# Splitting the next heads' weights at the ends of steps instead of in the middle of one

## The chip, the core and the metric

The kernel runs on one core of a Trainium2 chip. Its engines work side by side, each from a queue of its own in the order in which the instructions were written: PE (TensorE) multiplies matrices; its weight loads are listed as PEld. DVE (VectorE) and ACT (ScalarE) work element by element and are the ones that read PE's results out of PSUM. POOL (GpSimd) works element by element on SBUF. SP (SyncE) only issues transfers (DMAs) here; ACT and POOL issue some as well. An instruction that waits holds everything behind it in its own queue.

The metric is the device time of one execution in microseconds (us). A profiled execution is measured too, and its trace is where durations come from.

## The reference: what is computed

The input `x` has 4 batches of 512 rows with 512 values. It is normalized row by row (layer norm); attention with 16 heads of size 128 and a feed-forward network with 1408 hidden units both read the normalized rows; the output is the input plus their product:

```python
xn = _layernorm(x, axis=-1)
s = _L0_attn_ref(xn, ...)          # q, k, v per head, causal softmax, z, sum over heads by W_O
g = _silu(_L0_ffn_ref(xn, ...))    # silu(gate) * up, then down
x = x + s * g
```

Only the attention half is touched by the change. Everything is float32.

## The kernel before, in words

**Split operands.** PE is fed in a rounded type (fp32r), which keeps fewer bits than float32. So each operand is held as a pair, a high part and a low part, and a product is made of three matmuls: high x high, low x high, high x low. To *split* a weight tile of 128 x 512 means: ACT copies it into the rounded type (the cast, line 154), and POOL subtracts that from the raw tile to get the low part (line 155). The raw tile comes from HBM into one of four buffers (pool `rawp`, function `stage`, line 150), issued from ACT's queue during the head steps.

**Steps.** The heads are taken in groups of two (`HG = 2`), eight groups. The main loop of line 681 has 64 steps: for each group g, for each batch b (4), for each head i of the group (2). Step n is 8g + 2b + i. In step n, in the order of PE's queue:

- the scores of this head, `sc` (lines 362 to 368), 128 rows at a time. DVE adds the mask and takes the row maxima (line 376), ACT takes the exponentials (line 390), DVE the reciprocals of the row sums (line 393), POOL normalizes (line 396). That is function `softmax`.
- half of the "filling" work: in steps with i = 0 two row blocks of the values `v` (`project_v`, lines 308 and 312, read out by ACT at line 318 and DVE at 319 and 320), in steps with i = 1 two row blocks of the output projection of the previous batch (`project_out`, lines 93 to 95, read out by DVE at 536).
- the queries and keys of the *next* step's head, `psq` and `psk` (line 105, read out by ACT at 333 and DVE at 334).
- `z` of the *previous* step's head (function `attend`, lines 477 to 481): its softmax, turned, times `v`. In steps 10 to 61 the first six matmuls need only the high part of the turned softmax, and the seventh is the first that reads the low part.
- the other half of the filling work.

The turned softmax takes a way round: DVE transposes 32 x 32 blocks (line 410), SP writes them to HBM (`turn`, line 415) and reads them back in another order (`ptr`, line 421), and in the next step `split_p` makes the pair `pt`: ACT casts two halves (line 443), and the low parts are subtracted at line 445, in steps 9 to 61 the first half by POOL and the second by DVE. In DVE's queue line 445 stands behind the row maxima, the reciprocals, the reading out of the first filling work and the six transposes of the step.

**When weights are loaded and split.** `prepare` issues the load and puts the split on a list with a step at which it is due; `split_pending(n)` makes all splits with a due step up to n, one after another, in the queues of ACT and POOL at the place where it is called. Per group g:

| weights | load issued in step | due | uses of the old weights end in |
|---|---|---|---|
| `wq`, `wk` of the next group's even head | 8g+3 | 8g+6 | 8g+5 |
| `wv` of the next group | 8g+5 | 8g+7 | 8g+6 |
| `wq`, `wk` of the next group's odd head | 8g+6 | 8g+7 | 8g+6 |
| `wo` of this group (g > 0) | 8g+1 | 8g+2 | 8g+1 |

The `wo` of group 0 is loaded in step 0 and due in step 1. Each row is two tiles, so two splits. `split_pending(n)` is called in the middle of step n, between the softmax and its split on one side and the queries of the next head on the other; in step 8g+7 it makes four splits.

Loads are issued after the keys of the step have been read out by ACT, that is behind line 333 in ACT's queue, together with the loads of the sums `a` (line 511) and of weights that a side job (`chores`, one piece a step) looks through. The chores' POOL additions (line 581) come every fourth step, 8g+1 and 8g+5.

Of the kernel before, what the change touches and what calls it, by code (L numbers as in the profile page):

```python
# [19 lines left out]
HG = 2  # L20
# [22 lines left out]
def kernel(  # L43
# [69 lines left out]
    with ExitStack() as at:  # L113
# [39 lines left out]
        def split_w(dst, raw):  # L153
            nc.scalar.copy(dst.hi, raw)
            return lambda on: on.tensor_tensor(dst.lo, raw, dst.hi32, ALU.subtract)

        def flat(s):
            return Split(s.hi.rearrange("p c e -> p (c e)"), s.lo.rearrange("p c e -> p (c e)"))

        def weight(pool, shape, name, tag):  # L160
            return Split(
                pool.tile(shape, F32R, name=name + "h", tag=tag + "h"),
                pool.tile(shape, F32R, name=name + "l", tag=tag + "l"),
            )
# [5 lines left out]
        def split_pending(n, on=nc.gpsimd):  # L170

            lows = []
            for due, dst, raw in [p for p in pending if p[0] <= n]:
                lows.append(split_w(dst, raw))
                if on is not None:
                    lows[-1](on)
            pending[:] = [p for p in pending if p[0] > n]
            return lows

        def prepare(due, dst, src, name):  # L180

            pending.append((due, dst, stage(src, name)))

        def prepare_qk(h, due, due_k=None):
            for d, src, n, when in ((wq, w_q, "wq", due), (wk, w_k, "wk", due_k or due)):
                d[h] = weight(wqkp, [P, ND, E], f"{n}{h}", n)
                prepare(when, flat(d[h]), src[h].rearrange("p c e -> p (c e)"), f"{n}r{h}")
# [11 lines left out]
        def prepare_o(g, due):  # L199
            wo[g] = weight(wvop, [P, HG, D], f"wo{g}", "wo")  # L200
            for i in range(HG):
                prepare(due, wo[g][:, i, :], w_o[g * HG + i], f"wor{g}_{i}")
# [19 lines left out]
        def ln_sd(b, tt):  # L222
            mv = mv_of.pop((b, tuple(tt)))
            sd = small.tile([P, len(tt)], F32, name="sd")
            nc.scalar.activation(sd, mv[:, :, 1], AF.Sqrt, bias=eps)
            sd_of[b] = mv, sd
            for k, t in enumerate(tt):
                ln_of[b, t] = mv[:, k, :], sd[:, k : k + 1]
# [13 lines left out]
        def ln_scales(b):  # L242

            mv, sd = sd_of.pop(b)
            rstd = small.tile([P, NT], F32, name="rstd4", bufs=2)
            nc.vector.reciprocal(rstd, sd)
            add = small.tile([P, NT], F32, name="shift", bufs=2)
            nc.vector.scalar_tensor_tensor(add, mv[:, :, 0], -1.0, rstd, ALU.mult, ALU.mult)
            scaled[b] = rstd, add
# [264 lines left out]
        def project_out(g, b, t, zTs):  # L514
            for step in project_out_steps(g, b, t, zTs):
                step()
# [93 lines left out]
        with tc.manual_schedule():  # L610
# [70 lines left out]
            for n, (g, b, i) in enumerate(heads):  # L681
                h = g * HG + i
                nxt = heads[n + 1] if n + 1 < len(heads) else None
                gb = g * B + b
                prev = divmod(gb - 1, B) if gb > 0 else None

                ln_next = g == 0 and i == 0 and b + 1 < B
                ln_b = None
                if g == 0 and (b, i) == (0, 0):
                    ln_b = 1  # L690
                if g == 0 and i == HG - 1 and b + 2 < B:
                    ln_b = b + 2

                def fill(ks):
                    for t in ks:
                        if i == 0 and not (n == 0 and t < 2):
                            project_v(g, b, t)
                        if i == HG - 1 and prev is not None:
                            project_out(*prev, t, zs[prev])


                early = n < HG * HG or nxt is None

                norms = []
                if ln_next:
                    norms = [lambda: ln_scales(b + 1)] + [
                        lambda t=t: ln_normalize(b + 1, t, t < NT // 2 if n > 0 else t == NT - 1)
                        for t in ((2, 3, 0, 1) if n > 0 else range(NT))
                    ]
                of = softmax(qT, kT, norms if n > 0 else [])  # L710
                if n > 0 and early:
                    pt = split_p(raw, B * HG < n < len(heads) - 2)
                half = NT // 2 if nxt is not None else NT - 1
                fill(range(0, half))
                if n > 0:
                    while norms:
                        norms.pop(0)()
                if n == 0:
                    ln_stats(ln_b, range(NT), slice(2, NT), mv)
                if nxt is not None:  # L720
                    raw_next = turn_p(of)
                if not early:
                    pt = split_p(raw, B * HG < n < len(heads) - 2)
                if n != HG:
                    split_pending(n)
                if nxt is not None:
                    if ln_b is not None and n > 1:
                        ln_stats(ln_b, range(NT))
                    nh = nxt[0] * HG + nxt[2]
                    if n == 0:  # L730
                        ln_sd(ln_b, range(NT))
                        table(AF.Exp)
                        while norms:
                            norms.pop(0)()
                    *_, qT = project(nxt[1], nh, wq[nh], bq_sb, "q")
                if nxt is not None:
                    *_, kT = project(nxt[1], nh, wk[nh], bk_sb, "k")
                    if n == HG:
                        split_pending(n)
                    raw = raw_next  # L740

                if prev is not None:
                    cut = NT // 2 if n + HG < len(heads) else NT - 1
                    for t in range(cut) if i == 0 else range(cut, NT):
                        load_acc(*prev, t)
                if nxt is None:

                    a_last = wvop.tile([P, NT, D], F32, name="a_last", tag="wv")
                    for t in range(NT):
                        load_acc(g, b, t, a_last[:, t, :])  # L750
                per_g = B * HG
                if (b, i) == (0, HG - 1 if g > 0 else 0):
                    prepare_o(g, n + 1)
                if g + 1 < NG:

                    if (b, i) == (1, HG - 1):
                        prepare_qk((g + 1) * HG, (g + 1) * per_g - 2)
                    if (b, i) == (2, HG - 1):
                        prepare_v(g + 1, (g + 1) * per_g - 1)
                    if (b, i) == (B - 1, 0):  # L760
                        prepare_qk((g + 1) * HG + 1, (g + 1) * per_g - 1)
                if g > 0:
                    next(chore)
                if before is not None:
                    attend_last(before, pt)
                if n == 1:
                    ln_stats(ln_b, range(NT))
                if ln_b is not None and n > 0:
                    ln_sd(ln_b, range(NT))
                    table(AF.Exp)  # L770
                if ln_next:
                    side.extend([lambda: None] * (2 * ND))
                    for t in range(NT):
                        side.extend(ln_transposes(b + 1, t))
                        side.append(lambda t=t: ln_low(b + 1, t))
                    fill(range(half, NT))
                    while side:
                        side.pop(0)()
                    if b + 2 < B:
                        for t in range(NT):  # L780
                            load_x(b + 2, t)
                if nxt is None:
                    pt = transpose_p(of)
                if not ln_next:
                    fill(range(half, NT))
                before = g, b, i
                if n == len(heads) - 2:
                    flag = nc.values_load(inexact, min_val=0, max_val=P * LOW_BITS)
                if n == len(heads) - 4:
                    assert found  # L790
                    low = low_bits()
                if n == len(heads) - 3:
                    inexact = any_of(low)
# [567 lines left out]
```

## Time and profile before

| what | value |
|---|---|
| time, median of 3 runs | 1196.16 us (1195.70 to 1196.83) |
| profiled execution, its own time | 1200.96 us |
| its span in the trace | 1199.2 us |
| PE busy | 1186.0 us, 99% of the span |
| DVE, ACT, POOL busy | 940.2, 606.8, 460.6 us |
| mean granted TensorE clock | 0.998 of full speed |
| head steps 8 to 62 | 14.55 us (odd) and 14.67 us (even), a few longer |
| DMA | 236.73 MB, 197 GB/s on average |

How to read the rows: an instruction's row has its start and duration in us, its engine, line and operation, and out<-in by the program's names; `x4` counts instructions merged into one row, and a bracket at the end gives the engine's idle time before it and what ended that. A row of the waits has who waited for what, and then the total, the count and the longest in us. A row of busy time by stretch has the stretch, its length, then the busy us of PE, PEld, DVE, ACT and POOL with counts, the granted clock, the busy share of the DMA engines and GB/s. A row of a tile has the durations in ns, least, median and most, and the first and last start in us.

Step starts, taken from the first `sc` matmul of a step, are used throughout: step 18 begins at 279.06 us, step 23 at 352.26, step 26 at 401.41, step 58 at 869.17.

### The profile page before, as it was taken

How to read it: one execution, taken by the hardware profiler on the slowest of the kernel's cores; microseconds unless marked ns; L12 is line 12 of the kernel's file. 1: busy time of each engine (PE TensorE's matmuls, PEld its weight loads, DVE VectorE, ACT ScalarE, POOL GpSimd, SP SyncE). 2: the span in 40 equal slices, each digit the busy share in tenths (PEclk: the TensorE clock that was granted, in tenths of full speed). 3: DMA queues.
4: the chain of work that ended last, by engine and by line, in shares of the span. 5: the costliest groups of instructions: out<-in, count | busy, mean ns of one | idle time of the engine just before them, and what ended most of it. 6: DMA issues, size and time to landing. Idle time of an engine off the chain costs nothing.

```text
span 1199.2 us, 20208 instructions
## 1 busy us (share of the span) xinstructions
PE 1186.0 (99%) x6478; PEld 1037.7 (87%) x6478; DVE 940.2 (78%) x2485; ACT 606.8 (51%) x1455; POOL 460.6 (38%) x635
## 2 busy tenths in 40 slices
PE   9999999999998999999999999999999999999997
PEld 8888888888887888888888888888888888989896
DVE  7987777888778878887888788877777778959574
ACT  6764444555444445554544454445444454637372
POOL 3312342444243424442544244325232364636250
PEclk9999999999999999999999999999999999999999
DMA  5555466756675667666756676666565698879691
GB/s 181 148 173 159 142 179 198 217 180 203 196 217 171 207 193 211 185 202 203 225 180 207 195 234 178 211 185 200 165 181 161 206 329 243 261 206 265 182 263 56
DMA packets 131505, 236.73 MB, mean 197 GB/s; under 512 B 14912, under 2 KB 58688, under 8 KB 131392
## 3 DMA queue, kind: packets, MB, share of 16 engines
q1 hardware_dynamic: 73584, 133.86, 36.3%
q10 hardware_dynamic: 29520, 53.40, 15.1%
q0 software_dynamic: 28288, 48.12, 14.2%
q8 instruction: 53, 0.87, 0.3%
q14 instruction: 60, 0.49, 0.1%
HBM read 150.51 MB, written 84.80 MB: 196 GB/s over the span
## 4 chain that ended last, share of the span: by engine, by line
PE 94%; DVE 3%; DMA 2%; ACT 1%; issue 0%; SPq 0%; ACTq 0%; DVEq 0%
PE psq L105 14%; PE psk L105 14%; PE psv L308 9%; PE z L477 8%; PE sc L105 8%; PE pd L1085 7%; PE px L915 6%; PE pso L93 5%; PE pso L94 5%; PE pso L95 5%; PE psv L312 4%; PE pz L915 3%; PE psv L105 2%; PE py L915 2%; DMA xt<-in_x 1%; PE pu L915 1%
## 5 line engine op out<-in xcount | busy, mean ns | idle before, releaser
L396 POOL TENSOR_SCALAR p<-p,rtot 128x512 f32<-128x512 f32 (+3 forms) x256 | 135.9, 550 | 567.5 <-DVE rtot L393 546.8
L390 ACT ACTIVATE p<-p,nmax 128x512 f32<-128x512 f32 (+3 forms) x256 | 140.8, 552 | 142.3 <-DVE nmax L376 142.3
L308 PE MATMUL psv<-wv,xh 128*128 128x512 f32 x448 | 124.7, 400 | 0.0
L410 DVE STREAM_TRANSPOSE sq<-p 128x256 f32<-128x256 f32 x378 | 113.4, 363 | 0.0
L105 PE MATMUL sc<-k,q 128*128 128x512 f32 (+2 forms) x576 | 112.4, 339 | 0.3 <-DVE k L334 0.3
L105 PEld LDWEIGHTS sc<-k,q 128*128 128x128 f32 x576 | 99.1, 188 | 11.4 <-DVE k L334 0.9
L376 DVE CUSTOM_DVE_ANT_0 p<-sc,mask 128x512 f32<-128x512 f32 (+2 forms) x192 | 96.3, 551 | 0.3 <-DVE v_3l L320 0.3
L333 ACT ACTIVATE k<-psk,consts 128x512 fp32r<-128x512 f32 (+1 forms) x65 | 44.2, 680 | 102.3 <-PE psk L105 102.3
L443 ACT CAST pt<-ptr 128x640 fp32r<-128x640 f32 x126 | 85.2, 725 | 13.7 <-DMA ptr<-turn 11.6
L445 POOL TENSOR_TENSOR pt<-ptr,pt 128x640 fp32r<-128x640 f32 x53 | 83.6, 1578 | 15.4 <-ACT pt L443 14.2
L308 PEld LDWEIGHTS psv<-wv,xh 128*128 128x128 f32 x448 | 76.1, 189 | 9.9
L334 DVE SCALAR_TENSOR_TENSOR k<-psk,consts,k 128x512 fp32r<-128x512 f32 (+1 forms) x65 | 48.1, 740 | 45.2 <-ACT k L333 45.0
L445 DVE TENSOR_TENSOR pt<-ptr,pt 128x640 fp32r<-128x640 f32 x73 | 79.4, 1098 | 2.6 <-ACT pt L443 2.5
L312 PEld LDWEIGHTS psv<-wv,xl 128*128 128x128 f32 x448 | 68.5, 189 | 9.4
L393 DVE RECIPROCAL rtot<-tot 128x1 f32<-128x1 f32 x256 | 41.6, 162 | 41.1 <-ACT p L390 34.7
L312 PE MATMUL psv<-wv,xl 128*128 128x256 f32 x448 | 71.0, 281 | 0.0
L536 DVE TENSOR_TENSOR a<-pso,a 128x512 f32<-128x512 f32 x108 | 69.7, 684 | 1.7 <-PE pso L95 1.0
L1085 PE MATMUL pd<-wd,hl 128*128 128x512 f32 (+1 forms) x187 | 69.8, 378 | 0.0
L1085 PE MATMUL pd<-wd,hh 128*128 128x512 f32 (+1 forms) x187 | 69.7, 378 | 0.0
L333 ACT ACTIVATE q<-psq,consts 128x512 fp32r<-128x512 f32 (+1 forms) x65 | 44.2, 680 | 33.4 <-PE psq L105 32.9
L904 POOL DMA_DIRECT2D ws<-sum x78 | 41.7, 543 | 37.6 <-PE px L915 34.5
L477 PE MATMUL z<-pt,v_0h 128*128 128x512 f32 x128 | 50.8, 397 | 3.6 <-DVE pt L445 3.6
(622 smaller groups left out, 3284.2 us busy)
## 6 DMA issues: line engine op xcount, KB each, us to landing
turn<-sq SPq DMA_DIRECT2D x63, 640.0 KB, 2.9
ptr<-turn SPq DMA_DIRECT2D x252, 160.0 KB, 5.3
acc<-a SPq DMA_DIRECT2D x124, 256.0 KB, 2.4
a<-acc ACTq DMA_DIRECT2D x108, 256.0 KB, 3.1
ws<-sum POOLq DMA_DIRECT2D x39, 384.0 KB, 5.0
wg<-in_gate_w POOLq DMA_DIRECT2D x44, 256.0 KB, 4.8
sum<-sums SPq DMA_DIRECT2D x22, 256.0 KB, 5.5
wu<-in_up_w POOLq DMA_DIRECT2D x44, 128.0 KB, 4.8
```

The lines of the kernel that those rows point to most:

```text
L105: nc.tensor.matmul(ps, l, r, start=n == 0, stop=n == len(todo) - 1)
L308: nc.tensor.matmul(ps, x_[c].hi, wv[g].both[:, :, c, :], start=c == 0, stop=False)
L312: nc.tensor.matmul(ps[:, 1], x_[c].lo, wv[g].hi[:, c, :], start=False, stop=c == ND - 1)
L333: nc.scalar.activation(q.hi[:, at_], ps, AF.Identity, bias=bias[:, h : h + 1])
L376: nc.vector.tensor_tensor_reduce(out=of[t], in0=where[t], in1=add, scale=-SCALE, scalar=BIG, op0=ALU.add, op1=ALU.min, accum_out=nmax[t],)
L390: nc.scalar.activation(of[t], of[t], AF.Exp, bias=nmax[t], scale=-1.0, accum_out=tot)
L396: nc.gpsimd.tensor_scalar(of[t], of[t], rtot, 1.0, ALU.mult, ALU.mult)
L410: nc.vector.transpose(dst.rearrange("p a s i -> p s a i"), src.rearrange("p (s a i) -> p s a i", s=n, i=Q),)
L445: on.tensor_tensor(dst(pt.lo), src, dst(pt.hi32), ALU.subtract)
L477: nc.tensor.matmul(o, v, p_, start=k == 0, stop=k == len(todo) - 1)
L915: nc.tensor.matmul(ps, l, r, start=not more and k == 0, stop=k == len(todo) - 1, skip_group_check=more,)
L1085: nc.tensor.matmul(self.ps, part, wd[f][:, self.c], start=f == 0 and part is h_.hi, stop=f == NF - 1 and part is h_.lo,)
```

## The change

`split_pending` is called once at the end of every step, with n + 1: what is due in the next step is split behind the last work of this one. The two calls in the middle go. The odd head's `wq` and `wk` become due one step later (8g+8 instead of 8g+7), so that the four splits of step 8g+7 are parted: `wv` at the end of step 8g+6, `wq` and `wk` at the end of step 8g+7. The `wo` of group 0 is due in step 2, so it is split at the end of step 1; the other `wo` are split at the end of step 8g+1, the step in which they are loaded.

```diff
                 if not early:
                     pt = split_p(raw, B * HG < n < len(heads) - 2)
-                if n != HG:
-                    split_pending(n)
...
                     *_, kT = project(nxt[1], nh, wk[nh], bk_sb, "k")
-                    if n == HG:
-                        split_pending(n)
                     raw = raw_next
...
                 if (b, i) == (0, HG - 1 if g > 0 else 0):
-                    prepare_o(g, n + 1)
+                    prepare_o(g, HG if g == 0 else n + 1)
...
                     if (b, i) == (B - 1, 0):
-                        prepare_qk((g + 1) * HG + 1, (g + 1) * per_g - 1)
+                        prepare_qk((g + 1) * HG + 1, (g + 1) * per_g)
...
                 if not ln_next:
                     fill(range(half, NT))
+
+                split_pending(n + 1)
                 before = g, b, i
```

In the order of the built program the counts of instructions on every engine are as before. On ACT and POOL the casts and subtractions of weights stand ahead of the next step's exponentials and normalizations; PE, DVE and SP keep their order, and so do the loads on ACT's queue.

## The prediction

> **What bounds the kernel now.** I read the page first, then the waits, then the tile `pt`, then the time line around the one long wait.
>
> ```profile
> span 1199.2 us, 20208 instructions
> PE 1186.0 (99%) x6478; PEld 1037.7 (87%) x6478; DVE 940.2 (78%) x2485; ACT 606.8 (51%) x1455; POOL 460.6 (38%) x635
> ```
>
> PE (TensorE) is the bound: 13.2 us of the span without a matmul. A change that only moves work of ACT and POOL can gain no more than what PE waits for, and lose whatever new wait it gives PE. In the head steps PE waits as follows.
>
> ```profile
> PE z L477 <- DVE pt L445: 3.6, 1, 3.6
> PE psq L105 <- ACT xh L283: 0.7, 1, 0.7
> PE sc L105 <- DVE k L334: 0.3, 2, 0.2
> ```
>
> One wait matters: 3.6 us, once, on `pt`, the low half of the turned softmax that DVE subtracts at L445. The tile view shows that this instruction usually takes 0.8 us and once took 5.4:
>
> ```profile
> L445 DVE TENSOR_TENSOR pt<-ptr,pt x73: 778/820/5442, 35.5 to 949.0; 128x640 fp32r<-128x640 f32 x73
> ```
>
> The time line of step 23 (the step in which four weights are split) shows why:
>
> ```profile
> 361.22 2.54 POOL L155 TENSOR_TENSOR wv<-wvr,wv 128x512 fp32r<-128x512 f32 x2
> 361.44 5.44 DVE L445 TENSOR_TENSOR pt<-ptr,pt 128x640 fp32r<-128x640 f32 x1
> 363.71 1.27 POOL L155 TENSOR_TENSOR wq7l<-wqr,wq7h 128x512 fp32r<-128x512 f32 x1
> 364.93 1.27 POOL L155 TENSOR_TENSOR wk7l<-wkr,wk7h 128x512 fp32r<-128x512 f32 x1
> 367.03 0.48 PE L477 MATMUL z<-pt,v_0h 128*128 128x512 f32 x1 [3.57 <-DVE pt L445]
> 369.97 0.63 PE L94 MATMUL pso<-wo2h,z5h 128*128 128x512 f32 x1
> 371.03 0.39 PE L94 MATMUL pso<-wo2h,z4h 128*128 128x512 f32 x1
> ```
>
> DVE's subtraction starts just after POOL's four weight subtractions and ends 0.7 us after the last of them: it sat through all four. Then PE's matmuls take 0.63 us instead of 0.39 for some 3.5 us; the granted clock is low there. Busy time by step gives the price: the step is 19.93 us long, where a step of its kind takes 14.55.
>
> ```profile
> 352.26:372.19 19.93, 16.36 (x72) 13.63 (x71) 17.24 (x37) 9.07 (x22) 8.55 (x9) 0.91 0.67 196
> 620.86:635.41 14.55, 14.55 (x73) 12.38 (x71) 11.50 (x33) 6.61 (x18) 6.89 (x9) 1.00 0.69 204
> ```
>
> So the stall costs 5.38 us: 3.57 idle and 1.81 of slow clock. Is it in the timed runs? The profiled execution took 1200.96 us, 4.80 above the median 1196.16 of the three. 1200.96 - 5.38 = 1195.58, at the lower end of the runs (1195.70 to 1196.83). I read this as: the stall is of the profiled execution and the timed runs had at most small ones. In six of the other steps with four splits DVE slipped in after one POOL instruction or before them (0.78 to 1.92 us), so the long block is a matter of chance.
>
> The Trainium skill, SBUF — State Buffer, section "Who interferes with whom", says that a DVE instruction with two SBUF inputs and a GpSimd instruction that reads SBUF exclude each other and that the later waits until the first *finishes*. The 5.44 us row disagrees: DVE waited for four. By the rule alone no block could exceed one POOL instruction (1.3 us) and the sum would start from 1195.58 as well.
>
> **The change part by part.** All instructions stay; eight splits per group (two each of `wq`/`wk` even, `wv`, `wq`/`wk` odd, `wo`) move in ACT's and POOL's queues. PE, DVE and SP keep their order, and the load issues on ACT's queue stay where they were.
>
> *Removed: the splits in the middle.* No weight subtraction of POOL now meets L445. The 5.38 us of step 23 cannot come from them any more, nor 0.3 us of small stalls (step 30: 14.87 instead of 14.67; step 18: 14.73). What is late next in these steps: nothing, since PE has no gap in the other steps.
>
> *Added: q/k and v splits at the ends of steps 8g+5, 8g+6, 8g+7.* Two ACT casts, 1.04 us of ACT's queue (they follow each other by 0.52), stand before the next step's exponentials. Cover: ACT idles 2.27 to 2.29 us there for the row maxima. Their loads landed a step earlier. POOL's two subtractions (2 x 1.29) fall into its 7.5 to 9 us of idle time and end 0.5 us or more before the first normalization. Cost 0. With the cover gone: 1.04 us later exponentials, which still leave `pt` 0.5 us early.
>
> *Added: the first `wo` at the end of step 1.* It stands behind the load of the Exp table, without idle time: the exponentials of step 2 start 1.04 us later, and so does L445 behind them, ending at 51.41 instead of 50.37; PE wants it at 51.26. With 0.14 from end to matmul, 0.3 us. It cancels the 0.3 above.
>
> *Added: the other `wo`, loaded and split in one step, 8g+1.* This is the part that costs. The load is issued some 11.5 us into a step of 14.55; before, the cast came 6 us into the next step, now it stands at the end of the same step, and ACT's queue is in order: a cast that waits for its load holds the next step's exponentials. Step 58, time line of ACT, DVE and PE before:
>
> ```profile
> 865.65 0.94 ACTq L150 DMA_DIRECT2D wor<-in_w_o  x2
> 868.49 0.40 ACT L489 ACTIVATE z14h<-rest,consts 128x128 fp32r<-128x128 f32 x1 [1.01 <-DVE rest L501]
> 871.18 0.73 ACT L390 ACTIVATE p<-p,nmax 128x512 f32<-128x512 f32 x1 [2.29 <-DVE nmax L376]
> 876.15 1.13 ACT L154 CAST wo7h<-wor 128x512 fp32r<-128x512 f32 x2
> 877.27 0.78 DVE L445 TENSOR_TENSOR pt<-ptr,pt 128x640 fp32r<-128x640 f32 x1
> 880.27 0.40 PE L477 MATMUL z<-pt,v_0h 128*128 128x512 f32 x1
> ```
>
> The tile view of `wor` in that stretch gives issue to landing, least, median and most (of two: first and second half):
>
> ```profile
> DMA to landing us min/median/max: 6.8/7.6/8.3
> ```
>
> Second half: issued 866.14, landed 874.43, 5.25 us into step 58 (it begins at 869.17). Now the chain of the step, in us from its start. The second cast can begin 0.08 after the landing and the exponentials follow 0.52 later: landing + 0.60. Then ACT's exponentials, DVE's reciprocals, four subtractions of `v` and six transposes: L445 begins 6.10 after the first exponential (871.18 to 877.27; 6.09 in step 26 too). It takes 0.78 and PE follows after 0.14. PE wants it at 11.10 (880.27). POOL's second subtraction ends about 1.4 after the first exponential could start, when the normalizations would begin (1.43 after, 872.61 in step 58), so it adds nothing. Stall = landing + 0.60 + 6.10 + 0.78 + 0.14 - 11.10 = landing - 3.48.
>
> Landings of the second half in steps 10, 18, 26, 34, 42, 50, 58, read the same way: 0.70, 4.30, 3.36, 3.89, 2.81, 3.40, 5.25. Stalls: 0, 0.82, 0, 0.41, 0, 0, 1.77. Sum 3.0 us. With every transfer 0.5 us sooner 1.6, 1 us sooner 0.8, 0.5 later 5.3, 1 later 8.1. No stall reaches the 3.57 us that cost clock, so each costs itself.
>
> The Trainium skill, DMA: Bandwidth & Descriptors, "Rules for kernel authors", speaks against this part: issue early, wait late. Its section "Anatomy of one DMA — SWDGE (gpsimd) path" prices a transfer at 2.0 us plus bytes over 436 GB/s, for another path than this one; 2.6 us for 256 KB would be an estimate under which nothing waits and the sum were 1195.6. The rows (4.8 to 8.3 us) decide.
>
> **Sum.** 1200.96 - 5.38 - 0.3 + 0.3 + 3.0 = 1198.6 us for a profiled execution. For timed runs, which I take to be without the stall, the same number: 2.4 us, 0.2%, above the median shown. 0.2% (2.4 us) is also about what a measurement of this kernel can tell from no change.
>
> **Rivals.**
> *Sooner landings.* The transfers of timed runs, without the profiler beside them, land 1 us or more sooner. Only step 58 stalls (0 to 0.8): 1195.6 to 1196.4, no change. For it: a sensitivity of almost 1 to 1, three of six steps within 0.5 us of the limit. Against: the transfers that share the window (`a`, `ptr`, `wor`) are the kernel's own.
> *The stall was in the timed runs.* One mechanism: DVE starved by four back-to-back POOL subtractions, in all timed runs. Then they lose 5.38 and gain 3.0: 1196.16 - 2.4 = 1193.8; it decides if the profiler itself costs some 5 us. For it: 1.13 us of spread among the runs allows all or none. Against: 1195.58 fits them without it.
> *Later landings.* A later exponential shifts later writes and loads, and all six `wo` land 1 us later: 8.1 us, 1195.6 + 8.1 = 1203.7.
> That the splits stay in place is excluded: the order of the built program shows them moved.
>
> **How the numbers follow.** The computed case 0.42 (own range 1197.2 to 1200.9, from half a us sooner or later), sooner 0.23, stall in the timed runs 0.21, later 0.14. Of the computed case two thirds lie above +0.2% (0.28) and with the later landings that is 0.42 slower. Faster: all of the third, 0.21, and 0.01 of the second. The rest, 0.36, is within 0.2%. The range leaves out half of the later case and the lower third of the third: 1192.8 to 1203.2.
>
> **What would show it.** No L445 on DVE over 1.5 us in steps 8g+6 and 8g+7, and all these steps at 14.55 or 14.67. In steps 8g+2 ACT's cast of `wo` waits for `wor`, with the exponential 0.6 after the landing, and steps 18, 34, 58 are longer by 0.4 to 1.8. I would be wrong if the `wo` casts found their data landed, if a lag in step 8g+2 carried on into 8g+3 (ACT's waits for `ptr` there), or if timed runs fell by 5 us.

## The result and the profile after

The changed kernel takes 1202.21 us (median of 6 runs, 1201.29 to 1205.60) against 1196.08 us for the kernel before on the same chip (1195.70 to 1196.95): a ratio of 1.0054, 95% interval 1.0041 to 1.0067. It is slower by 6.1 us. The profiled execution of the changed kernel took 1201.54 us, one of the six.

The page of the changed kernel, the span and the engines:

```profile
span 1199.8 us, 20214 instructions
PE 1185.8 (99%) x6478; PEld 1035.7 (86%) x6478; DVE 915.8 (76%) x2485; ACT 609.6 (51%) x1455; POOL 449.1 (37%) x635
```

DVE is 24 us and POOL 12 us less busy than before, and nothing is gained: they are not the bound. PE's waits:

```profile
PE z L477 <- DVE pt L445: 4.1, 6, 1.3
PE z L477 <- ACT pt L443: 0.3, 1, 0.3
```

One wait of 3.6 us has become six of up to 1.3, on the same tile `pt`. But L445 itself is no longer long; its tile row (least, median and most in ns) ends at 1309 where it ended at 5442:

```profile
L445 DVE TENSOR_TENSOR pt<-ptr,pt x73: 775/783/1309, 35.5 to 949.9; 128x640 fp32r<-128x640 f32 x73
```

So it now starts late. Busy time by step shows where: step 23, then steps 2 and 4, then the six steps 8g+2 from 18 on.

```profile
355.01:369.57 14.56, 14.56 (x73) 12.38 (x71) 12.21 (x37) 8.67 (x22) 6.16 (x7) 1.00 0.75 237
...
39.19:57.87 18.68, 17.63 (x114) 15.32 (x112) 16.76 (x44) 13.92 (x28) 6.13 (x6) 1.00 0.33 105
72.63:90.26 17.63, 17.15 (x113) 15.31 (x111) 14.56 (x39) 11.08 (x24) 2.40 (x4) 1.00 0.52 145
280.96:296.54 15.58, 14.88 (x79) 12.77 (x78) 12.46 (x37) 7.74 (x19) 6.23 (x7) 1.00 0.59 182
398.79:414.13 15.34, 14.88 (x80) 12.75 (x78) 11.89 (x34) 7.55 (x19) 6.21 (x7) 1.00 0.63 181
516.34:531.01 14.67, 14.67 (x80) 12.76 (x78) 12.35 (x36) 8.01 (x20) 6.18 (x7) 1.00 0.74 203
633.22:648.64 15.42, 14.87 (x79) 12.74 (x78) 11.90 (x34) 7.74 (x19) 6.21 (x7) 1.00 0.61 187
750.89:767.10 16.21, 14.89 (x80) 12.76 (x79) 12.50 (x37) 7.74 (x19) 6.21 (x7) 1.00 0.58 177
869.31:884.73 15.42, 14.89 (x80) 12.76 (x78) 10.99 (x34) 8.00 (x20) 6.23 (x7) 1.00 0.53 163
```

Against the profiled execution of before: step 23 is 5.4 us shorter, steps 2 and 4 together 1.9 longer (18.68 and 17.63 instead of 17.23 and 17.15), and the steps 8g+2 from 18 to 58 take 0.91, 0.67, 0, 0.75, 1.54 and 0.75 us more than 14.67: 4.6 in all, at full clock (the column 1.00). That is +1.1 in these steps, and the span grew by 0.6, against an execution that had a 5.4 us stall in it; the timed runs of before do not have that stall, and so lose all of it.

The time line of step 18 of the changed kernel, ACT, DVE and PE, shows the new wait whole:

```profile
283.70 0.62 ACT L154 CAST wo2h<-wor 128x512 fp32r<-128x512 f32 x1 [1.64 <-DMA wor<-in_w_o]
285.37 0.62 ACT L154 CAST wo2h<-wor 128x512 fp32r<-128x512 f32 x1 [1.05 <-DMA wor<-in_w_o]
285.89 0.72 ACT L390 ACTIVATE p<-p,nmax 128x512 f32<-128x512 f32 x1
...
291.99 0.78 DVE L445 TENSOR_TENSOR pt<-ptr,pt 128x640 fp32r<-128x640 f32 x1
292.91 0.47 PE L477 MATMUL z<-pt,v_0h 128*128 128x512 f32 x1 [0.70 <-DVE pt L445]
```

ACT stands idle for the two halves of `wor`; the first exponential comes 0.52 us after the second cast began, L445 6.10 us after that, and PE 0.14 after its end: each link has the length that the prediction gave it.

The time line of step 2, POOL, DVE and PE, shows the other loss:

```profile
46.49 2.54 POOL L155 TENSOR_TENSOR wo0l<-wor,wo0h 128x512 fp32r<-128x512 f32 x2 [9.27 <-ACT wo0h L154]
47.95 1.09 DVE L248 SCALAR_TENSOR_TENSOR shift<-mv,rstd 128x4 f32<-128x4 f32 x1
49.00 3.62 POOL L396 TENSOR_SCALAR p<-p,rtot 128x512 f32<-128x512 f32 x4
49.04 0.94 DVE L264 TENSOR_SCALAR xn<-xt,mv,rstd 128x512 f32<-128x512 f32 x1
50.42 0.50 PE L477 MATMUL z<-pt,v_0h 128*128 128x512 f32 x1 [0.35 <-ACT pt L443]
50.70 1.76 DVE L445 TENSOR_TENSOR pt<-ptr,pt 128x640 fp32r<-128x640 f32 x2
52.51 0.50 PE L477 MATMUL z<-pt,v_0h 128*128 128x512 f32 x1 [0.55 <-DVE pt L445]
```

The same instructions in the profile before, where step 2 begins at 39.21 us (here at 39.19):

```profile
46.92 3.61 POOL L396 TENSOR_SCALAR p<-p,rtot 128x512 f32<-128x512 f32 x4 [7.18 <-DVE rstd L246]
46.93 0.18 DVE L248 SCALAR_TENSOR_TENSOR shift<-mv,rstd 128x4 f32<-128x4 f32 x1
47.34 0.56 DVE L264 TENSOR_SCALAR xn<-xt,mv,rstd 128x512 f32<-128x512 f32 x1
48.75 1.62 DVE L445 TENSOR_TENSOR pt<-ptr,pt 128x640 fp32r<-128x640 f32 x2
```

A DVE instruction on 128x4 elements (the shift of the layer norm) takes 1.09 us instead of 0.18: it ends 0.02 us after POOL's second subtraction of the first `wo`. The next one, on 128x512, takes 0.94 instead of 0.56. No subtraction runs beside it any more; it begins together with POOL's first normalization and ends 0.28 us after it. (Before, it began later in that normalization and ended 0.28 us after it too.) L445 ends at 52.46, 13.27 us into the step instead of 11.16.

### The profile page after: what moved, and what is told of

Same layout as the page of the kernel before. It is cut to its first block, busy times and chain, and to the rows that moved or that the text cites. A ratio compares the mean times of both kernels' runs of the same rounds, so it can differ in the third digit from the quotient of the medians.

```text
span 1199.8 us, 20214 instructions
## 1 busy us (share of the span) xinstructions
PE 1185.8 (99%) x6478; PEld 1035.7 (86%) x6478; DVE 915.8 (76%) x2485; ACT 609.6 (51%) x1455; POOL 449.1 (37%) x635
## 4 chain that ended last, share of the span: by engine, by line
PE 88%; DMA 4%; DVE 3%; ACT 2%; issue 1%; ACTq 0%; SPq 0%; POOL 0%; DVEq 0%
PE psq L105 13%; PE psk L105 13%; PE psv L308 8%; PE z L477 8%; PE sc L105 7%; PE pd L1083 7%; PE px L913 6%; PE pso L93 5%; PE pso L94 4%; PE pso L95 4%; PE psv L312 4%; PE pz L913 3%; DMA wor<-in_w_o 2%; PE psv L105 2%; PE py L913 2%; ACT p L390 1%
## 5 line engine op out<-in xcount | busy, mean ns | idle before, releaser
L443 ACT CAST pt<-ptr 128x640 fp32r<-128x640 f32 x126 | 85.3, 726 | 11.3 <-DMA ptr<-turn 9.2
L445 POOL TENSOR_TENSOR pt<-ptr,pt 128x640 fp32r<-128x640 f32 x53 | 83.7, 1579 | 10.8 <-ACT pt L443 10.4
L536 DVE TENSOR_TENSOR a<-pso,a 128x512 f32<-128x512 f32 x108 | 69.8, 685 | 3.1 <-DMA a<-acc 3.1
L445 DVE TENSOR_TENSOR pt<-ptr,pt 128x640 fp32r<-128x640 f32 x73 | 60.9, 845 | 2.9 <-ACT pt L443 2.9
```

The costliest lines, as they stand in the source:

```text
L445: on.tensor_tensor(dst(pt.lo), src, dst(pt.hi32), ALU.subtract)
```

## The experiments

The theory after the result: all of the loss comes from the `wo` splits and none from the `wq`, `wk` and `wv` splits. The later `wo` cost what the landing of their load is late; the first `wo` costs through POOL's subtractions, which hold normalizations and DVE. Rivals: ACT's casts ahead of the exponentials cost wherever they stand; or the order of the loads does.

### The `wq`, `wk`, `wv` splits alone

The changed kernel with all `wo` splits back in the middle of the step, each due as before. A second list keeps them apart:

```diff
-        def split_pending(n, on=nc.gpsimd):
+        other = []
+        def split_pending(n, on=nc.gpsimd, pending=pending):
...
-                prepare(due, wo[g][:, i, :], w_o[g * HG + i], f"wor{g}_{i}")
+                (other if True else pending).append((due, wo[g][:, i, :], stage(w_o[g * HG + i], f"wor{g}_{i}")))
...
                     pt = split_p(raw, B * HG < n < len(heads) - 2)
+                split_pending(n, pending=other)
...
-                    prepare_o(g, HG if g == 0 else n + 1)
+                    prepare_o(g, n + 1)
```

> The change with every wo split put back where it was (middle of steps 1 and 8g+2); wq, wk and wv are split at the ends of steps. Theory (the loss is wo's: 4.5 us of waiting for its load in steps 18 to 58 and 1.9 us in steps 2 and 4): 1195.3 to 1196.1 us, as the kernel before or up to 0.6 us below it, all steps 8 to 60 at 14.55 or 14.67 us. Rival (casts and subtractions at the end of a step cost by standing ahead of the exponentials and normalizations, whichever weight it is): 23 of the 29 pairs are still there, so 1200 us or more.

Measured: 1196.03 us (1195.1 to 1197.1), ratio to before 1.0005, 95% interval 0.9995 to 1.0014. PE's wait for L445 is down to one:

```profile
PE z L477 <- DVE pt L445: 0.2, 1, 0.2
```

It belongs to step 18, which takes 15.05 us and not the expected 14.67; there L445 takes 1.38 us and stands next to the `wo` split in the middle of the step, as in the kernel before. All other steps from 8 to 60 have their usual length to within 0.1 us. Moving and parting the other six splits of a group costs nothing and gains nothing that can be measured.

### The `wo` splits alone

The kernel before, with only the `wo` splits moved to the ends of steps (same second list, called at the end of the step):

```diff
-                    prepare_o(g, n + 1)
+                    prepare_o(g, HG if g == 0 else n + 1)
...
                     fill(range(half, NT))
+                split_pending(n + 1, pending=other)
```

> The kernel before with the wo splits alone moved to the ends of steps 1 and 8g+1; wq, wk, wv stay in the middle, four at once in steps 8g+7. Theory: all of the loss, 1201.3 to 1203 us, with L445 of steps 18, 26, 42, 50 and 58 late by the landing less 3.5 us. Rival (position): 6 of 29 pairs moved, so about 1197.3 us.

Measured: 1200.17 us, ratio 1.0044, interval 1.0030 to 1.0057; 1.1 us under what was expected, and 2.9 over the rival. In its profile steps 2 and 4 are 2.4 us longer than in the profile before, and the steps 18 to 58 lose 3.25 us. The two experiments split the change cleanly: the loss goes with `wo`.

### The load one step earlier

The changed kernel, with the load of `wo` issued in step 8g and its split left at the end of step 8g+1:

```diff
-                prepare(due, wo[g][:, i, :], w_o[g * HG + i], f"wor{g}_{i}")
+                pending.append((due, wo[g][:, i, :], raws[i]))
...
+                if (b, i) == (0, 0):
+                    raws = [stage(w_o[h + k], f"wor{g}_{k}") for k in range(HG)]
                 if (b, i) == (0, HG - 1 if g > 0 else 0):
-                    prepare_o(g, HG if g == 0 else n + 1)
+                    prepare_o(g, HG if g == 0 else n + 1, raws)
```

> The change with the load of wo issued one step earlier (step 8g in place of 8g+1), the splits left at the end of step 8g+1. Theory (the cast waits for the transfer, nothing else): steps 18 to 58 fall back to 14.67, 4.5 us go and 1.9 us of steps 2 and 4 stay: 1197.4 to 1198 us. Rival (position, with the data long there): unchanged, 1202 us.

Measured: 1198.13 us, ratio 1.0020, interval 1.0011 to 1.0029; the expected range ended at 1198. All six steps from 18 to 58 are back at 14.66 or 14.67 us, with the same ACT casts ahead of the same exponentials: these casts cost nothing, the wait for the load does. What is left is in steps 2 and 4. PE's wait for L445 that remains is the one of step 2:

```profile
PE z L477 <- DVE pt L445: 0.5, 1, 0.5
```

### The first `wo` back in the middle

The changed kernel, with the split of the first `wo` alone back in the middle of step 1 (the second list for g = 0 only, due and called there as in the kernel before):

```diff
+                (other if g == 0 else pending).append((due, wo[g][:, i, :], stage(w_o[g * HG + i], f"wor{g}_{i}")))
```

> The change with the first wo alone split in the middle of step 1 again. Theory: steps 2 and 4 get back their 1.45 and 0.48 us, 1202.2 - 1.9 = 1200.3 us. Rival (steps 2 and 4 differ for another reason, such as the earlier transfers of q and k): unchanged, 1202 us.

Measured: 1198.59 us, ratio 1.0025, interval 1.0014 to 1.0036. One of the eight executions took 6737.08 us, which nothing on record explains; it is not in the ratio, and without it the median is 1198.33, 2.0 us less than expected. Steps 2 and 4 take 17.54 and 16.85 us, so this loss is gone; the other stalls remain, 4.0 us in the profiled execution (1199.01 us). That the size was missed fits stalls that vary from one execution to the next, as the next table has it; the executions that were only timed have no trace, so this is not shown for them.

### Stall against landing

Four kernels load and split the later `wo` in one step. For the six steps 8g+2 from 18 on, the landing of the second half (us from the start of the step, read from the trace as in the prediction) and the excess of the step over its least length, 14.66 us:

| step | after | `wo` splits alone | first `wo` in the middle | subtractions behind (below) |
|---|---|---|---|---|
| 18 | 4.38: 0.92 | 4.89: 1.44 | 4.33: 0.87 | 3.66: 0.20 |
| 26 | 4.13: 0.68 | 2.23: 0.01 | 3.81: 0.34 | 3.51: 0.07 |
| 34 | 3.29: 0.01 | 3.58: 0.11 | 3.70: 0.24 | 3.34: 0.00 |
| 42 | 4.23: 0.76 | 4.05: 0.58 | 3.44: 0.00 | 3.30: 0.01 |
| 50 | 5.01: 1.55 | 4.10: 0.64 | 4.61: 1.15 | 5.08: 1.61 |
| 58 | 4.21: 0.76 | 3.92: 0.47 | 4.84: 1.38 | 3.41: 0.01 |
| sum | 4.7 | 3.25 | 4.0 | 1.9 |

In all 24 cells the excess is the landing less 3.48, or nothing, to within 0.04 us; in 17 of them the landing lies far enough above 3.48 for a stall of 0.1 us or more. The landings scatter, the rule does not. They scatter in the kernel before as well: with those of its second profile (below) the rule gives 3.6 us, where the prediction had 3.0 from the first.

### POOL's subtractions behind the normalizations

The changed kernel; ACT casts the first `wo` at the end of step 1 as before, but POOL's two subtractions come behind the normalizations of step 2:

```diff
+                if n == 2:
+                    for low in late:
+                        low(nc.gpsimd)
                 fill(range(0, half))
...
-                split_pending(n + 1)
+                late = split_pending(n + 1, None if n == 1 else nc.gpsimd)
```

> Against after only one thing is changed: the two POOL subtractions of the first `wo` no longer stand ahead of the normalizations of step 2 in POOL's queue but behind them; ACT's two casts (1.04 us) stay at the end of step 1. In after, steps 2 and 4 together are 1.9 us longer than in before. Theory: it is POOL's two subtractions (2.54 us) that cost it, since the normalizations wait behind them and two small VectorE instructions beside them (L248, L264) took 0.9 and 0.4 us more than usual. Then steps 2 and 4 lose 0.3 to 0.5 us in all, VectorE's L248 takes about 0.2 us again, the normalizations begin some 8.7 us into step 2 instead of 9.8, and the time falls by 1.4 to 1.6 us against after (1200.0 to 1201.0). Rival: ACT's casts alone delay the exponentials and all behind them; then steps 2 and 4 still lose 1.9 us or more and the time stays at 1202.

Measured: 1200.14 us, ratio 1.0039, interval 1.0026 to 1.0053, where the changed kernel had 1.0054: the expected size, though the intervals overlap. The trace decides. The two DVE instructions in the time line of step 2 have their old lengths:

```profile
48.66 0.18 DVE L248 SCALAR_TENSOR_TENSOR shift<-mv,rstd 128x4 f32<-128x4 f32 x1
49.07 0.55 DVE L264 TENSOR_SCALAR xn<-xt,mv,rstd 128x512 f32<-128x512 f32 x1
```

Step 4 is back at 17.15 us, its length in the first profile of before. Step 2 takes 18.38, 0.30 less than after. How much is that worth? In the profiles with the first `wo` in the middle (before, twice, and three of the other kernels) steps 2 and 4 together take 34.4 to 34.6 us. With all of it at the end (the changed kernel and three others) they take 36.3 to 36.8. Here they take 35.5. So POOL's subtractions make 0.8 to 1.3 us of a loss of 1.8 to 2.4, and about 1.0 us stays with ACT's casts: more than the expected 0.3 to 0.5, less than the rival's 1.9. Of this 1.0, a wait of PE of 0.23 us for `pt` of L443 is seen. PE also waits 0.56 us for `q` at the start of step 2, before the edit can act; kernels with the first `wo` in the middle do so too (0.22 to 0.47 in four profiles) and are at most 0.2 us longer for it over the two steps. The rest of the 1.0 us is not traced. The normalizations began 9.30 us into the step, not at the expected 8.7, for the same late start.

### The load ahead of the others

The changed kernel, with the loads of `wo` put ahead of the loads of the sums `a` in ACT's queue, in the same step:

```diff
+                if (b, i) == (0, HG - 1 if g > 0 else 0):
+                    prepare_o(g, HG if g == 0 else n + 1)
                 if prev is not None:
...
-                if (b, i) == (0, HG - 1 if g > 0 else 0):
-                    prepare_o(g, HG if g == 0 else n + 1)
```

> Against after, the two loads of `wo` are issued in the same step as there, but ahead of the loads of `a` in ACT's queue instead of behind them, some 0.8 to 1.5 us sooner. Theory (the stall of a step 8g+2 is the landing of the second half, in us from the step's start, less 3.48): the landings come 0.8 to 1.5 us sooner, so 2.9 to 3.6 us into the steps; the stalls sum to 0.3 to 1.5 us instead of 4.6, and in each step stall and landing keep the difference of 3.48; the time is 1198.6 to 1200.4 with steps 2 and 4 unchanged. Rival (the exponentials are late for ACT's casts themselves, not for the load): nothing changes, 1201.3 or more, and the stalls no longer follow the landings.

Measured: 1207.82 us, ratio 1.0094, interval 1.0078 to 1.0109. Both expectations fell: it is slower than the changed kernel too. The profiled execution is the slowest of the five, 1213.51 us, so its stalls are larger than those of the others. In it `wor` did land sooner than expected, 0.9 us before the start of the step to 0.5 after it, and no cast waited. But now the two tiles of `a` are last. The waits of DVE, the time line of DVE and ACT in step 18 (start 281.87), and that step by busy time:

```profile
DVE a L536 <- DMA a<-acc: 17.9, 13, 2.6
```

```profile
288.14 0.69 DVE L536 TENSOR_TENSOR a<-pso,a 128x512 f32<-128x512 f32 x1 [1.09 <-DMA a<-acc]
288.75 0.68 DVE L376 CUSTOM_DVE_ANT_0 p<-sc,mask 128x512 f32<-128x512 f32 x1
...
289.54 0.72 ACT L390 ACTIVATE p<-p,nmax 128x512 f32<-128x512 f32 x1 [5.18 <-DVE nmax L376]
```

```profile
281.87:301.72 19.85, 16.68 (x80) 14.01 (x78) 13.96 (x40) 8.25 (x22) 6.16 (x7) 0.91 0.64 172
```

L536, the readout of the output projection, adds `a`, and it stands ahead of the row maxima in DVE's queue. It waits for `a`, the row maxima wait behind it, and the exponentials for them. The second `a` lands 3.4 to 6.2 us into the step instead of within 1.0 us of its start, and stall is landing of `a` less 2.5 in four of the six steps (26, 42, 50, 58: 4.05, 3.40, 4.53, 3.94 give 1.51, 0.89, 2.01, 1.41). In steps 18 and 34 it is 1.5 us more; in both the granted clock is 0.91 over the step and PE is busy for 16.7 us instead of 14.9. The waits of PE that came before were of 1.56 to 1.58 us; one of 1.58 in step 50 left the clock at 1.00. So the stall belongs to whichever load is last in line, and `a` has less room than `wo`. Order within the step only chose the victim; issuing a step earlier removed it.

### Both losses taken away

Load of `wo` one step earlier and the first `wo` in the middle of step 1, the two edits above together:

> After with both of its losses taken away: the first `wo` is split in the middle of step 1 as in before, and the load of the other `wo` is issued one step earlier, in step 8g, with the split still at the end of step 8g+1. If the two losses are all that the change costs, the time is that of before, 1195.4 to 1196.4, with steps 2 and 4 and all steps 8g+2 at their usual length. Rival: two splits at the end of a step cost something by themselves in the steps where they stand; then the time stays above 1197. If before's timed runs had small stalls from four splits at once, it would be faster than before by up to 0.5 us.

Measured: 1195.84 us (1194.71 to 1197.83), before 1195.86 us; ratio 1.0003, interval 0.9994 to 1.0012. To within this interval the two losses are the whole cost of the change. And with them gone nothing is left over: what the change was to remove had no price in the timed runs. It does not beat the kernel before by a measurable amount. The comparison also gives the size of each loss in timed runs. With the load early and the first `wo` at the end, the time was 1198.13, so the first `wo` costs 2.3 us, as in the profiles (steps 2 and 4 take 36.8 and 34.6 us in these two kernels). With the load late and the first `wo` in the middle it was 1198.33, so the later ones cost 2.5 us.

### The kernel before, looked at again

> Another look at the kernel before. Theory: the 5.38 us stall of step 23 in the first profiled execution was a chance event. Then step 23 takes 14.5 to 14.7 us here, no L445 on VectorE takes over 2 us, and the profiled execution takes 1195.5 to 1197. Rival: the profile brings the stall with it; then it takes about 1201 again, with a VectorE subtraction of 3 us or more in one of the steps with four splits.

Measured: 1195.87 us. Busy time of its step 23:

```profile
352.39:367.05 14.66, 14.66 (x72) 12.36 (x71) 13.29 (x34) 8.69 (x21) 9.26 (x9) 1.00 0.73 233
```

The longest L445 on DVE took 1.92 us, and PE did not wait for it once. None of the 48 times of before in this study, beside the first profiled execution, is above 1197.1 us. The 5.38 us stall was seen in that one execution alone.

### How long POOL can hold DVE

Two small kernels, each repeating the meeting of POOL's four subtractions with DVE. The core of the second one:

```python
for r in range(192):
    nc.scalar.copy(dst(pth), src)
    nc.scalar.copy(hi, raw)
    for k in range(4):
        nc.gpsimd.tensor_tensor(lows[k], raw, hi.bitcast(F32), ALU.subtract)
    for _ in range(r // 16 % 6 + 1):
        w = (r % 16 + 1) * 32
        nc.vector.transpose(sq[:, :w], hi.bitcast(F32)[:, :w])
    nc.vector.tensor_tensor(dst(ptl), src, dst(pth.bitcast(F32)), ALU.subtract)
    ...     # in the first 96 rounds: four loads of 256 KB
```

> This kernel copies the input to the output and leaves all of the computation out; beside that it repeats one situation 96 times: POOL runs four 128x512 subtractions back to back, and VectorE, after two transposes whose width changes from round to round, the 128x640 subtraction of two tiles in SBUF (as L445). Another 96 rounds have a 128x4 scalar_tensor_tensor (as L248) and a 128x512 tensor_scalar (as L264) instead. Theory of chance: where VectorE's subtraction arrives while POOL works, it mostly gets in after one POOL instruction (ends within 0.8 to 2.1 us of its start) and in a few per cent of the rounds it sits through several (3 us or more), as once in some thirty steps of before. Rival, the rule that the later one waits until the first is done: no subtraction of VectorE takes over 2.1 us. Second rival, POOL always keeps the way: most rounds take 3 us or more, and then the four splits in the middle would have cost in all of before's runs. Of the other 96: if the small instructions are held too, the 128x4 one takes up to 1.1 to 1.5 us instead of 0.18 in those rounds in which it meets POOL.

The tile rows of the first (least, median, most in ns):

```profile
L51 DVE TENSOR_TENSOR ptl<-ptr,pth x96: 825/1367/1369, 3.6 to 591.1; 128x640 fp32r<-128x640 f32 x96
...
L58 DVE SCALAR_TENSOR_TENSOR shift<-ones x96: 119/644/1166, 592.8 to 860.8; 128x4 f32<-128x4 f32 x96
...
L61 DVE TENSOR_SCALAR xn<-raw,ones x96: 532/1560/1564, 593.5 to 861.3; 128x512 f32<-128x512 f32 x96
```

The small instructions are held as the ones of step 2 were: the first takes 0.12 us when it is not held and up to 1.17 beside POOL, the second 0.53 in the four rounds behind POOL's last subtraction and 1.49 to 1.56 beside it. The subtraction never took over 1.37, but in nearly all rounds it arrived at the same moment, so this run could not tell the theory of chance from the rule.

> Like the run before it, this kernel only copies the input to the output and leaves all of the computation out. In that run VectorE's subtraction always arrived about 0.7 us into the first of POOL's four, so that one moment was tried 96 times. Here one to six transposes of changing width stand before it, which begin with POOL's first subtraction, so that it arrives anywhere from 0.2 to 4 us into the four, 192 times; in the first part of the rounds loads of 256 KB run beside it. Theory of chance: a few of the 192 sit through two or more POOL instructions (2.1 us and longer), as once in step 23 of before, where the subtraction arrived 0.2 us after the first. Rival, the rule that the later one waits only until the first is done: none is longer than 2.1 us at any moment of arrival, with loads or without, and the 5.44 us need something that these rounds lack.

```profile
L48 DVE TENSOR_TENSOR ptl<-ptr,pth x192: 781/1389/1898, 4.2 to 1206.4; 128x640 fp32r<-128x640 f32 x192
```

Here the arrivals run from 0.09 to 4.32 us into POOL's four. The duration falls along a saw: 1.85 us for an arrival at 0.09, 1.72 at 0.22, 0.78 at 1.20, up again to 1.90 at 1.27, and so on for each of POOL's instructions, the same with loads beside it and without. It is always the rest of the POOL instruction in progress plus some 0.7 us. The theory of chance falls for this pair of instructions: in 192 rounds none sat through two. DVE's turn shows on POOL's side too: in 184 rounds one of POOL's four takes over 1.8 us instead of some 1.26. In step 23 none of the four did (1.27 to 1.30), so DVE had no turn between them. The 5.44 us of step 23, where the arrival was at 0.22, needed something that these rounds lack. It was seen once and what it was stays open.

## Why the prediction was right or wrong, point by point

**Base without the stall (1200.96 - 5.38 = 1195.58).** Right: the second look took 1195.87 and had no stall. Why DVE sat through four subtractions in that one execution stays open. The rival that put the stall in the timed runs falls with it; nothing was gained by its removal.

**Small stalls of steps 18 and 30, minus 0.3.** In the second look both steps take 14.67 us, so these stalls too were of the first profiled execution. In the timed runs 0.3 us can't be told from the spread.

**`wq`, `wk`, `wv` splits at 0.** Right: ratio 1.0005 with these alone.

**First `wo`, 0.3 us.** This term failed: 1.9 us in the profile, 1.8 to 2.4 in four kernels. The prediction followed ACT's 1.04 us down to L445 and stopped there; it asked for the later `wo` whether POOL's subtractions delay the normalizations, and not for this one. POOL's two instructions pushed the normalizations of step 2 from 7.71 to 9.81 us into the step, and the second of them held the shift (0.91 us more). The next layer-norm instruction, which also stands ahead of L445, then met the first normalization (0.38 us more), and DVE's lag reached step 4, where PE waited 0.32 us for `q`. ACT's part was too small as well: with POOL's two instructions out of the way about 1.0 us was left, not 0.3. The Trainium skill, SBUF — State Buffer, section "Who interferes with whom", names both kinds: a DVE instruction with two SBUF inputs (the shift), and `tensor_scalar`, which can take a mode that uses both ports. The trace of step 2 agrees: the shift ended 0.02 us after POOL's subtraction, and the `tensor_scalar` 0.28 us after POOL's normalization. The prediction applied that rule to L445 alone, and there doubted it for a single row; the saw above agrees with it in 192 of 192 rounds.

**Later `wo`, 3.0 us by landing less 3.48.** The mechanism and its constant were right to 0.04 us in 24 steps. The size depends on the landings: 4.7 us in the profiled execution after, 3.25, 4.0 and 1.9 in three others. The 3.0 lies inside that scatter, but an execution's landings from before were taken as if they were fixed. The times can't confirm this scatter by themselves: six runs of the changed kernel lie within 4.3 us and six of before within 1.25, but 24 runs of before lie within 3.1, and eleven of the kernel with the early load, where no cast waits, within 3.9. That no stall would cost clock was right here (clock 1.00, waits of PE up to 1.3 us); but waits of 1.56 to 1.58 us did in two steps of the kernel with the load ahead, so the 3.57 us that the prediction compared with is no safe limit.

**The sum, 1198.6.** The measured 1202.21 lies 3.6 above the number, and the loss of 6.1 us is two and a half times the forecast 2.4. It lies above the range given for the computed case, 1197.2 to 1200.9; the wide range up to 1203.2 holds it only because of room left for later landings, and so partly by luck. With the terms as measured: 1195.87 + 1.8 (steps 2 and 4 against the second look) + 4.6 (steps 18 to 58) = 1202.3; the profiled execution of after took 1201.54, and some 0.6 us less lie behind the last head step, which no run explains. Of the 3.6, some 1.5 are the first `wo`, 1.6 later landings than assumed, and 0.6 the base (1195.87 instead of 1195.58 - 0.3). In timed runs of the kernels with one loss each, the two cost 2.3 and 2.5, together 4.8 us; both together took 6.1 in the changed kernel and 4.5 in the kernel with the `wo` splits alone. The scatter of the landings can make such differences; that it made these is not shown.

**Rivals.** "Sooner landings" (1195.6 to 1196.4) did not happen; the landings of the profiles and the time of the runs fit each other. "Later landings" (8.1 us of stalls, 1203.7) points the right way, but the largest sum in a profile was 4.7; its time was nearly reached because the first `wo` cost what it did.

**The skill's rule on loads.** The Trainium skill, DMA: Bandwidth & Descriptors, "Rules for kernel authors", issue early and wait late, spoke against this part of the change, and the load one step earlier agrees: a ratio of 1.0020 instead of 1.0054.

## What to carry to other kernels

A split, cast or copy that consumes a load should not be moved ahead of critical work in an in-order queue unless the load moves as well or has landed by then; its price is the lateness of the landing, and that price scatters, so take it from more than one execution. When an instruction is moved on one engine, follow every engine that it feeds or shares a port with up to the same point, the small instructions too. When a profile shows a stall, compare the time of its own execution with the other runs: if it is longer by just that stall, as here (4.80 and 5.38 us), there is nothing to win in the others.

## What was not expected of the hardware

- POOL's 128x512 subtraction can stretch a DVE instruction of 128x4 elements from 0.18 to 1.09 us (0.12 to 1.17 in the small kernel): what counts is how much of the POOL instruction is left, not the length of DVE's.
- The 128x640 subtraction of DVE got in after one POOL instruction at every moment of arrival tried, at most 1.90 us for an instruction of 0.78; four in a row were no worse than one. POOL's next one then took over 1.8 us instead of 1.26. The single 5.44 us is unexplained.
- After waits of PE of 1.56 to 1.58 us the granted clock fell to 0.91 over the step in two steps (18 and 34) and stayed at 1.00 in one (50); after waits of up to 1.41 us in these steps it did not fall.
- Of two loads in one queue in the same step, changing the order moved the second `a` from within 1.0 us of the step's start to 3.4 to 6.2 us into it, and the second half of `wor` from 3.3 to 5.0 us into the step to between 0.9 us before its start and 0.5 after.
